# The key projection of a graph attention kernel by features instead of by edges, and a changed first stage

## The chip, the cores and the metric

The kernel runs on one core of one Trainium2 chip. The metric is the device time of one execution in microseconds. Before the change three runs took 2660.58, 2667.97 and 2672.92 us, with the median 2667.97. One further execution was profiled: 2659.95 us.

## The reference

12500 nodes with 128 features, 212500 edges sorted by their destination `dst`. Attention has 8 heads of 16 features:

```
h = relu(layernorm(x))
q = h @ Wq.T + bq ;  v = h @ Wv.T + bv              # per node
k = edge_attr @ Wk.T + bk                            # per edge
qs, qd = q[src], q[dst]
in_m, out_m, diag_m = sum(qs*k), sum(qd*k), sum(qs*qd)   # per head
score = (softmax(in_m/4) + softmax(out_m/4) + softmax(diag_m/4)) * edge_weight**lam
h = segment_sum(score * v[dst], dst)                 # the softmaxes run over the edges of one dst
out = x + leaky_relu(h @ Wo.T + bo, 0.1)
```

The input lam is 1.0, and the kernel skips the power when it is.

## The kernel before

**Cutting up the edges.** The edges are cut into 415 blocks of 512 (128 partitions by 4 columns, JN = 4) and 20 edges left over, the "few". The blocks form S = 5 streams of G = 83 blocks. The loop (line 1754) takes one block of each stream in turn, so five iterations g make one cycle t, s = g % 5.

**The first stage** (to about 157 us in the profile) normalizes the nodes, multiplies them by Wq and writes the query table to DRAM (L1017, L1021). It turns the destinations into bf16 numbers that later make the one-hot matrices, and loads weights and biases. SP's queue carries most of its transfers. It also begins GpSimd's work: indirect gathers fetch the source's row for each edge, four DMAs of 128 rows per block (L713), from the raw x for the first 24 blocks and from the query table afterwards. 29 blocks are gathered ahead of the loop, and then the 20 edges left over, with one gather for their sources and one for their destinations (L743).

The key bias is handled in the first stage. A reflection per head (`bring_to_size`, `reflect`, small VectorE operations and a square root on ScalarE) turns the features of q and of k alike, which leaves their products unchanged, in such a way that the bias of each head falls into one feature, its "lead". Wq, Wk and bq are turned with it.

**The loop, per block g.** The order on each engine is the order in which the code is written: `pin` chains every instruction to the one before it on the same engine.
- TensorE: `turn(g+2)` transposes a block of edge features into PSUM (`eT_ps`, one buffer), ScalarE copies it (`eT`, three buffers). `project(g+1)` multiplies: four matmuls with a slice of eT as the stationary operand and Wk moving, each in two passes (float32), and one small bf16 matmul that adds the lead bias (L1329). k stands in PSUM with edges on partitions (`k_ps`, two buffers). `spread_q(g+1)` selects the destinations' queries by four one-hot matmuls (`qd_ps`, two buffers), which ScalarE copies to `qd`.
- ScalarE: the eT copy, two activations that make the one-hots for g+3 (L704, L705), the qd copy (L1340).
- VectorE: `logits(g)`, three products into one tile of 128x1536 (L1348 qs*k, L1349 qs*qd, L1350 qd*k) and one reduction (L1351).
- A tail that depends on s: scans for the running maxima, exponentials, and w_ps, the weighted sums (L1507), for cycles t-1 to t-3.
- GpSimd: `gather(g+26)`, four DMAs. Line 717 holds them behind TensorE: rows 0 and 1 wait for the last instruction of `project(g)`, issued in the iteration before (`behind[g, 0]`), and rows 2 and 3 wait for the last TensorE instruction of the tail of that iteration (`behind[g, 2]`).
- SP: one load of edge features (`ea`, six buffers, 256 KB), windows of the query table, and stores.

Two iotas on GpSimd (L1698, L1700) at g = 4 and an operation at g = 7 make the selection matrix `shows`.

The lines behind these names:

```
713   rows = pin(nc.gpsimd.indirect_dma_start(out=qq[:, j, :], ...
717   held = behind.get((g - LOOK, j), held)          # LOOK = 26
1320  transpose(eT_ps[:, j, :], ea ...)     1322 eT <- eT_ps (ScalarE)
1328  matmul(k_ps[:, j, :], eT[:, j, :], wk)  1329 k_ps += bias of the leads
1337  matmul(qd_ps[:, j, :], one-hot, window) 1340 qd <- qd_ps (ScalarE)
```

## Time and profile before

| | before |
|---|---|
| three runs | 2660.58, 2667.97, 2672.92 us |
| profiled execution | 2659.95 us, its span 2658.2 us |
| granted TensorE clock, mean | 0.756 |
| gathers from the query table (L713) | 1564, 947 ns each |
| block reduction (L1351) | 415, 1753 ns each |

The first row of the page gives busy time, share of the span and number of instructions of each engine: PE is TensorE's matmul, PEld its weight loads (they overlap with matmuls), DVE is VectorE, ACT ScalarE, POOL GpSimd. In the groups, "busy, mean of one | idle time of the engine just ahead of them, and what ended most of it" follows the shapes. "issue" is time in which an engine waited for nothing that the profile shows; "remote" in the waits is a release that the profile can't name. TensorE's clock changes between 0.5 and 1.0 of full speed during the execution.

### The profile page before, as it was taken

What the parts mean: (1) busy time and instruction counts of PE and PEld (TensorE: products, weight loads), DVE (VectorE), ACT (ScalarE), POOL (GpSimd) and SP (SyncE); (2) the same over time, 40 slices, a digit from 0 to 9 for tenths busy, and PEclk for the clock granted to TensorE, in tenths of its full rate; (3) what the DMA queues carried; (4) which work ended last, traced back from release to release, by engine and by line L of the source; (5) the groups of instructions that cost most, each with busy time, mean ns of one, the idle gap of its engine ahead of it and who ended that gap; (6) DMA issues with size and microseconds to landing.
All of it is one profiled execution on the core that took longest, in us unless ns stands there. A gap on an engine that the chain in (4) does not pass through costs nothing.

```text
span 2658.2 us, 37064 instructions
## 1 busy us (share of the span) xinstructions
PE 1798.2 (68%) x10958; PEld 1457.9 (55%) x10958; DVE 2037.4 (77%) x2835; ACT 1408.4 (53%) x2744; POOL 1587.1 (60%) x1683
## 2 busy tenths in 40 slices
PE   3766766666667667666676677667767676677785
PEld 2455655555555555555555555555555565556674
DVE  4658877777777778787777877777877787777995
ACT  3657754554455555554555555555555555555672
POOL 6655666666666666666666666666666666666100
PEclk7778878777777777776777777777777777667786
DMA  6665455455545554455445544554455445454431
GB/s 187 171 188 156 126 130 145 130 135 137 146 134 136 141 149 128 137 144 145 119 128 134 139 123 130 133 135 126 124 135 131 131 131 132 132 137 123 126 88 53
DMA packets 379842, 357.08 MB, mean 134 GB/s; under 512 B 193358, under 2 KB 299640, under 8 KB 379426
## 3 DMA queue, kind: packets, MB, share of 16 engines
q1 hardware_dynamic: 310720, 239.37, 32.0%
q0 software_dynamic: 53184, 108.92, 16.8%
q10 hardware_dynamic: 15728, 6.33, 1.0%
q8 instruction: 90, 1.47, 0.2%
q14 instruction: 120, 0.98, 0.1%
HBM read 322.16 MB, written 32.22 MB: 133 GB/s over the span
## 4 chain that ended last, share of the span: by engine, by line
PE 44%; issue 16%; DVE 14%; ACT 14%; another core or an unknown queue 8%; DVEq 1%; DMA 1%; POOL 0%; ACTq 0%; SPq 0%
PE k_ps L1328 12%; PE eT_ps L1320 8%; PE w_ps L1507 7%; PE qd_ps L1337 4%; PE m_ps L1451 3%; ACT qd L1340 3%; ACT eT L1322 2%; DVE prod L1349 2%; DVE lT L1351 2%; PE node_ps L1259 2%; DVE prod L1350 2%; DVE prod L1348 2%; ACT relb L704 2%; PE k_ps L1329 2%
## 5 line engine op out<-in xcount | busy, mean ns | idle before, releaser
L713 POOL DMA_INDIRECT qq<-q_table,sources x1564 | 1480.4, 947 | 846.4 <-issue 359.4
L1351 DVE TENSOR_REDUCE lT<-prod 128x96 f32<-128x1536 f32 x415 | 727.4, 1753 | 14.3
L1328 PE MATMUL k_ps<-wk,eT 128*128 128x128 f32 x3320 | 609.4, 341 | 63.5 <-issue 32.2
L1320 PE MATMUL eT_ps<-ident,ea 128*128 128x128 f32 x1660 | 349.4, 345 | 384.1 <-issue 260.9
L1328 PEld LDWEIGHTS k_ps<-wk,eT 128*128 128x128 f32 x3320 | 556.5, 252 | 93.2 <-issue 46.7
L1340 ACT COPY qd<-qd_ps 128x512 f32<-128x512 f32 x415 | 239.5, 577 | 536.2 <-remote 154.7
L1320 PEld LDWEIGHTS eT_ps<-ident,ea 128*128 128x128 f32 x1660 | 240.2, 175 | 479.4 <-issue 315.1
L1348 DVE TENSOR_TENSOR prod<-qq,k_ps 128x512 f32<-128x512 f32 x412 | 280.4, 681 | 206.4 <-PE eT_ps L1320 51.7
L1322 ACT COPY eT<-eT_ps 128x512 f32<-128x512 f32 x415 | 242.8, 585 | 261.3 <-remote 125.3
L1349 DVE TENSOR_TENSOR prod<-qq,qd_ps 128x512 f32<-128x512 f32 x412 | 281.4, 683 | 92.9 <-ACT qd L1340 57.5
L704 ACT ACTIVATE relb<-relb,before 126x512 bf16<-126x512 bf16 x415 | 302.6, 729 | 0.0
L1507 PE MATMUL w_ps<-back,sel 128*126 128x144 f32 (+1 forms) x1296 | 207.8, 325 | 113.3 <-ACT sel L1497 86.1
L1350 DVE TENSOR_TENSOR prod<-qd,k_ps 128x512 f32<-128x512 f32 x415 | 281.8, 679 | 0.0
L705 ACT ACTIVATE oh<-relb 126x512 bf16<-126x512 bf16 x415 | 261.4, 630 | 13.2
L1507 PEld LDWEIGHTS w_ps<-back,sel 128*126 128x126 f32 (+1 forms) x1296 | 189.9, 218 | 126.7 <-ACT sel L1497 96.9
L1337 PE MATMUL qd_ps<-win,oh 126*128 126x128 bf16 x1660 | 199.6, 252 | 16.0 <-issue 14.7
L1337 PEld LDWEIGHTS <-oh 126*128 126x128 bf16 x1660 | 112.2, 109 | 41.3 <-issue 16.9
L1460 DVE TENSOR_TENSOR back<-lT,m_ps 128x480 f32<-128x480 f32 x83 | 54.0, 651 | 93.5 <-remote 36.4
L1451 PE MATMUL m_ps<-ident,m 120*128 120x120 f32 x332 | 74.4, 359 | 67.0 <-issue 39.7
L1411 DVE TENSOR_TENSOR_SCAN l_ps<-far,carry,l_ps 120x512 f32<-120x512 bf16 x80 | 102.5, 1281 | 20.7 <-PE h_ps L1379 6.7
L713 POOL DMA_INDIRECT qq<-in_x_dram,sources x84 | 81.4, 969 | 46.9 <-issue 22.4
L1439 DVE TENSOR_TENSOR_SCAN m<-far,head,l_ps 120x512 f32<-120x512 bf16 x81 | 102.9, 1270 | 0.0
(263 smaller groups left out, 1802.6 us busy)
## 6 DMA issues: line engine op xcount, KB each, us to landing
ea<-in_edge_attr_dram SPq DMA_DIRECT2D x415, 256.0 KB
relb<-rel_d SPq DMA_DIRECT2D x83, 630.0 KB
qq<-q_table,sources POOLq DMA_INDIRECT x1564
win<-q_table SPq DMA_DIRECT2D x415, 31.5 KB
far<-far_d SPq DMA_DIRECT2D x84, 135.0 KB
q_table<-q SPq DMA_DIRECT2D x24, 384.0 KB
sums<-rows SPq DMA_DIRECT2D x411, 7.9 KB
q_table<-xq SPq DMA_DIRECT2D x24, 256.0 KB
```

Of the source, the lines that this page charges most:

```text
L704: pin(nc.scalar.activation(d, d, AF.Abs, bias=before[:K3]))
L713: rows = pin(nc.gpsimd.indirect_dma_start(out=qq[:, j, :], out_offset=None, in_=x if g < RAW else q_table, in_offset=bass.IndirectOffsetOn ...
L1320: pin(nc.tensor.transpose(eT_ps[:, j, :], eas[g][:, j * F:(j + 1) * F], ident))
L1322: pin(nc.scalar.copy(eT, eT_ps))
L1328: pin(nc.tensor.matmul(k_ps[:, j, :], eTs[g][:, j, :], wk, start=(j == 0), stop=False))
L1337: pin(nc.tensor.matmul(qd_ps[:, j, :], ohs[g][:, j * P:(j + 1) * P], d["win"][:, s, :], start=(j == 0), stop=(j == JN - 1)))
L1340: pin(nc.scalar.copy(qds[g], qd_ps))
L1348: pin(nc.vector.tensor_mul(prod[:, :, 0, :], qqs[g], ks[g]))
L1349: pin(nc.vector.tensor_mul(prod[:, :, 1, :], qqs[g], q_ps[g]))
L1350: pin(nc.vector.tensor_mul(prod[:, :, 2, :], qds[g], ks[g]))
L1351: pin(nc.vector.tensor_reduce(lTs[t][:, :, s, :], prod.rearrange("p j i (h d) -> p j (i h) d", d=DIM), AX.X, ALU.add))
L1507: pin(nc.tensor.matmul(w_ps[:(hi - lo) * W, lo:hi].rearrange("p s c -> p (s c)"), d["sel"][:n, j, lo:hi, :].rearrange("p s w -> p (s w)"), ...
```

## The change

**In the loop** the projection runs the other way. `project` is one matmul with Wk as the stationary operand and all 512 columns of eT moving, and gives k by features, `kT_ps` (features on partitions, one PSUM buffer). ScalarE copies it with `bk` as a bias per partition. `turn_back` then transposes it by four matmuls into `k_ps`, with edges on partitions as before. So the reflection is gone, with the matmul for the bias. PSUM has one buffer for each of eT_ps, kT_ps and qd_ps, and two for k_ps; eT has two buffers in SBUF instead of three. An iteration runs turn_back(g+1), spread_q(g+1), project(g+2) and turn(g+3), and the hold for gather rows 0 and 1 stands behind spread_q(g+1). The qs*qd product is VectorE's first of the three.

**In the first stage** lam is loaded as one number (the broadcast load is inside the branch that is skipped), the nine loads of block bounds move to iterations 1 to 6 of the loop, and the loads of biases and bases move to other turns. The selection matrix comes from two small VectorE operations on an index table instead of the two iotas. The few edges are gathered by one DMA of 40 rows, and SP moves the second 20 in iteration 1.

TensorE's order for one iteration in the loop, s = 4, names as in the lists above; before the change:

```order
L1320 MATMUL eT_ps<-ident,ea 128x128 x4
L1328 MATMUL k_ps<-wk,eT 128x128 x4
L1329 LDWEIGHTS ones_92
L1329 MATMUL k_ps<-b_98,ones_92 128x32
L1337 LDWEIGHTS oh
L1337 MATMUL qd_ps<-win,oh 128x128
...
L1507 MATMUL w_ps<-back,sel 126x144 x4
L1507 MATMUL w_ps<-back,sel 84x96 x4
L1371 MATMUL l_ps<-ident,lT 120x128 x4
```

and in the same place after it (L1283 is `turn_back`, L1290 `spread_q`, L1275 `project`, L1268 `turn`):

```order
L1283 MATMUL k_ps<-ident,kT 128x128 x4
L1290 LDWEIGHTS oh
L1290 MATMUL qd_ps<-win,oh 128x128
...
L1275 MATMUL kT_ps<-eT,wk 128x512
L1268 MATMUL eT_ps<-ident,ea 128x128 x4
L1460 MATMUL w_ps<-back,sel 126x144 x4
L1460 MATMUL w_ps<-back,sel 84x96 x4
L1324 MATMUL l_ps<-ident,lT 120x128 x4
```

The transpose of edge features moved from the front of an iteration to the place ahead of the tail; k for the next block, made of ScalarE's kT, stands in front.

ScalarE's order for the iterations s = 3 and s = 4, before:

```order
L1322 COPY eT<-eT_ps 128x512
L704 ACTIVATE relb<-relb,before 126x512
L705 ACTIVATE oh<-relb 126x512
L1340 COPY qd<-qd_ps 128x512
L1496 ACTIVATE sel<-d_ps 128x420 x2
L1497 ACTIVATE sel<-sel 128x840
```

and after:

```order
L705 ACTIVATE relb<-relb,before 126x512
L706 ACTIVATE oh<-relb 126x512
L1293 COPY qd<-qd_ps 128x512
L1278 ACTIVATE kT<-kT_ps,bk_col 128x512
L1270 COPY eT<-eT_ps 128x512
L1449 ACTIVATE sel<-d_ps 128x420 x2
L1450 ACTIVATE sel<-sel 128x840
```

The eT copy moved behind the qd copy, and the new kT copy stands between them.

GpSimd's order at the end of the first stage, before:

```order
L713 DMA qq<-q_table,sources 128x128 x20
L743 DMA qq<-q_table,few_i 20x128 x2
L713 DMA qq<-q_table,sources 128x128 x8
L1698 IOTA ends_ab 21x840
L1700 IOTA ends_ab 1x840
L713 DMA qq<-q_table,sources 128x128 x1536
```

and after:

```order
L859 UNCONDITIONAL_BRANCH x2
L714 DMA qq<-in_x_dram,sources 128x128 x40
L714 DMA qq<-q_table,sources 128x128 x20
L755 DMA qq<-q_table,few_i 40x128
L714 DMA qq<-q_table,sources 128x128 x1544
```

One gather of 40 rows stands where two of 20 stood, and the two iotas are gone from between the loop's gathers.

The core of the diff:

```diff
-    bk_lead = b3[:, 1, None, 0::DIM].to_broadcast([3, JN, HEADS])
+    show_end = consts.tile([K4, S * JN], F32, name="show_end")
+    nc.vector.tensor_scalar(show_end, jp[:K4, 1:K4], 0.0, -1.0, op0=ALU.is_equal, op1=ALU.mult)
+    show_row = consts.tile([1, W], F32, name="show_row")
+    nc.vector.tensor_copy(show_row, jp[0:1, 1:W + 1])
...
-        for i in range(2):
-            pin(nc.gpsimd.indirect_dma_start(
-                out=few["q"][:, i, :], out_offset=None, in_=q_table,
-                in_offset=bass.IndirectOffsetOnAxis(ap=few["i"][:, i:i + 1], axis=0)))
+        pin(nc.gpsimd.indirect_dma_start(
+            out=rows[:, 0, :], out_offset=None, in_=q_table,
+            in_offset=bass.IndirectOffsetOnAxis(ap=few["i"], axis=0)))
+        return rows
+
+    def part_few(rows):
+        pin(nc.sync.dma_start(rows[:EL, 1, :], rows[EL:, 0, :]))
...
-        pin(nc.sync.dma_start(lam_sb, lam[None, :].to_broadcast([RW, 1])))
+        pin(nc.sync.dma_start(lam_sb[0:1, :], lam[None, :]))
...
         with tc.If(lam_v != 0x3F800000):
+            nc.sync.dma_start(lam_sb, lam[None, :].to_broadcast([RW, 1]))
...
-        side = {2: [load_b], 4: [load_bases], 8: [cast_dst], 9: [mark, mark_heads], 10: [store_far], 11: [near_due],
+        side = {5: [load_b], 8: [cast_dst], 9: [mark, mark_heads, load_bases], 10: [store_far], 11: [near_due],
...
-        for s in range(S + 1):
-            beside(12 + s, load_bounds, s)
...
-        bring_to_size()
...
-            if g == -2:
-                reflect()
...
-            eT = work.tile([P, JN, P], F32, name="eT", bufs=3)
+            eT = work.tile([P, JN, P], F32, name="eT")
...
         def project(g):
+            kT_ps = ps.tile([P, JN, P], F32, name="kT_ps", bufs=1)
+            pin(nc.tensor.matmul(kT_ps.rearrange("f j p -> f (j p)"), wk,
+                                 eTs.pop(g).rearrange("f j p -> f (j p)"), start=True, stop=True))
+            kTs[g] = work.tile([P, JN, P], F32, name="kT")
+            pin(nc.scalar.activation(kTs[g], kT_ps, AF.Identity, bias=bk_col))
+
+        def turn_back(g):
             k_ps = ks[g] = ps.tile([P, JN, F], F32, name="k_ps", bufs=2)
             for j in range(JN):
-                pin(nc.tensor.matmul(k_ps[:, j, :], eTs[g][:, j, :], wk, start=(j == 0), stop=False))
-            pin(nc.tensor.matmul(k_ps.rearrange("p j (h d) -> p j h d", d=DIM)[:, :, :, 0], ones3, bk_lead,
-                                 start=False, stop=True))
-            del eTs[g]
+                pin(nc.tensor.transpose(k_ps[:, j, :], kTs[g][:, j, :], ident))
+            del kTs[g]
...
-            qd_ps = q_ps[g] = ps.tile([P, JN, F], F32, name="qd_ps", bufs=2)
+            qd_ps = q_ps[g] = ps.tile([P, JN, F], F32, name="qd_ps", bufs=1)
...
+            pin(nc.vector.tensor_mul(prod[:, :, 1, :], qqs[g], q_ps[g]))
             pin(nc.vector.tensor_mul(prod[:, :, 0, :], qqs[g], ks[g]))
-            pin(nc.vector.tensor_mul(prod[:, :, 1, :], qqs[g], q_ps[g]))
...
         turn(0)
         project(0)
+        turn(1)
+        turn_back(0)
         spread_q(0)
-        turn(1)
+        project(1)
+        turn(2)
...
+            if g + 1 < end:
+                turn_back(g + 1)
+                one_hots(g + 3)
+                spread_q(g + 1)
+                behind[g + 1, 0] = pinned[products]
             if g + 2 < end:
-                turn(g + 2)
-            one_hots(g + 3)
-            if g + 1 < end:
-                project(g + 1)
-                behind[g + 1, 0] = pinned[products]
-                spread_q(g + 1)
+                project(g + 2)
+            if g + 3 < end:
+                turn(g + 3)
             logits(g)
...
+                if t == 0:
+                    part_few(rows_few)
...
-            if g == 4:
-                show_places()
-            elif g == 7:
+            if 0 < g <= S + 1:
+                load_bounds(g - 1)
+            if g == 7:
                 show()
```

More of the change, by code (lines that the diff above doesn't have):

```diff
@@ L972, in turn_w @@
         def turn_w(i, to):
             w_ps = prep_ps.tile([P, F], F32, name="t_ps")
-            if i in (0, 2):
-                pin(nc.tensor.matmul(w_ps, w_in[:, i, :], axes, start=True, stop=True))
-            else:
-                pin(nc.tensor.transpose(w_ps, w_in[:, i, :], ident))
+            pin(nc.tensor.transpose(w_ps, w_in[:, i, :], ident))
             pin(nc.scalar.copy(to, w_ps))
@@ L1868, in ordered_path @@
             halves_of(ab, engine)
-        places_o = [ps.tile([P, JN, F], F32, name="eT_ps", bufs=1)]
-        for r in range(2):
-            places_o += [ps.tile([P, JN, F], F32, name=name, bufs=2) for name in ("k_ps", "qd_ps")]
+        places_o = [ps.tile([P, JN, F], F32, name=name, bufs=n) for name, n in
+                    (("eT_ps", 1), ("kT_ps", 1), ("k_ps", 2), ("k_ps", 2), ("qd_ps", 1))]
         for r in range(len(rest) + 2):
```

101 lines of the change are left out of this document (26 added, 75 removed).

## The prediction

> **What bounds the kernel now.** I first read the page for the load of each engine.
>
> ```profile
> PE 1798.2 (68%) x10958; PEld 1457.9 (55%) x10958; DVE 2037.4 (77%) x2835; ACT 1408.4 (53%) x2744; POOL 1587.1 (60%) x1683
> L713 POOL DMA_INDIRECT qq<-q_table,sources x1564 | 1480.4, 947 | 846.4 <-issue 359.4
> ```
>
> No engine is full, VectorE at 77% the nearest to it, so no busy time explains the span, and I looked for a rate and for what sets it. One reduce (L1351, VectorE) ends the scores of each block, so its count in a window counts blocks. The columns are window, length, busy time, count, granted clock, DMA share, GB/s.
>
> ```profile
> 2000.00:2400.00 400.00, 120.93 (x69) 0.72 0.49 130
> 2500.00:2570.00 70.00, 27.75 (x16) 0.80 0.41 114
> 1700.00:1760.00 60.00, 17.44 (x10) 0.67 0.51 136
> 1450.00:1510.00 60.00, 17.53 (x10) 0.83 0.50 127
> ```
>
> A block takes 5.8 us in the loop (400 / 69), and 4.4 us in the window after 2500 (70 / 16). What is absent there is GpSimd's gathers, whose last is issued at 2477.69. TensorE's clock does not matter: a stretch at 0.67 and one at 0.83 both hold 10 blocks. The timeline of GpSimd and that of ScalarE show the coupling (start, length, then idle time before and what ended it).
>
> ```profile
> 2222.98 0.94 POOL L713 DMA_INDIRECT qq<-q_table,sources  x1 [1.74 <-PE qd_ps L1337]
> 2229.22 0.94 POOL L713 DMA_INDIRECT qq<-q_table,sources  x1 [0.30 <-issue]
> 2231.73 0.94 POOL L713 DMA_INDIRECT qq<-q_table,sources  x1 [1.57 <-PE m_ps L1451]
> 2477.69 0.95 POOL L713 DMA_INDIRECT qq<-q_table,sources  x1 [0.30 <-issue]
> ```
>
> ```profile
> 2222.68 0.41 ACT L1512 COPY rows<-w_ps 126x144 f32<-126x144 f32 x2 [3.74 <-PE qd_ps L1337]
> 2225.28 0.60 ACT L1322 COPY eT<-eT_ps 128x512 f32<-128x512 f32 x1
> 2231.55 0.59 ACT L1340 COPY qd<-qd_ps 128x512 f32<-128x512 f32 x1 [4.39 <-PE m_ps L1451]
> ```
>
> From 2222.98 to 2230.16 six gathers go out back to back, 1.25 us apart (0.94 and 0.30). The chain of waits for that stretch shows TensorE's side:
>
> ```profile
> 2223.63 0.66 PE eT_ps L1320 x4
> ...
> 2225.33 0.33 PE qd_ps L1337 x4
> 2225.94 0.65 PE eT_ps L1320 x4
> ...
> 2228.01 0.33 PE qd_ps L1337 x4
> 2228.34 1.34 issue
> ```
>
> The qd copy that ScalarE starts at 2231.55 needs the matmuls that ended at 2225.66, yet it starts 5.9 us later, after the row of gathers is over at 2230.16. So I read: while GpSimd issues gathers back to back, TensorE's completions reach the others late, and they come out together some 1.4 us after the last gather. GpSimd itself stops because its gathers are held behind TensorE (lines 717 to 721), so each round is some gathers and one stall. Before the loop the same is seen at full size: the 20 last gathers of the first stage and the two of L743 go out in one row that ends at 181.5, and the next scores start after it.
>
> ```profile
> 180.60 0.91 POOL L743 DMA_INDIRECT qq<-q_table,few_i  x1 [0.30 <-issue]
> 166.23 1.75 DVE L1351 TENSOR_REDUCE lT<-prod 128x96 f32<-128x1536 f32 x1
> 185.39 0.69 DVE L1348 TENSOR_TENSOR prod<-ends_ab,k_ps 128x512 f32<-128x512 f32 x1 [17.41 <-remote]
> ```
>
> The table of waits sizes the rounds (us in total, times, longest).
>
> ```profile
> POOL qq L713 <- issue: 381.8, 1242, 1.0
> POOL qq L713 <- remote: 130.5, 76, 2.9
> POOL qq L713 <- PE qd_ps L1337: 83.4, 55, 2.2
> POOL qq L713 <- PE eT_ps L1320: 65.4, 45, 2.3
> POOL qq L713 <- PE k_ps L1329: 63.4, 33, 4.8
> POOL qq L713 <- PE m_ps L1451: 32.4, 22, 1.8
> POOL qq L713 <- PE h_ps L1379: 21.8, 19, 1.7
> ```
>
> The "issue" row is the ordinary step, 381.8 / 1242 = 0.31 us. The other six are stalls: 250, together 396.9 us, 1.59 each, or 1.29 above the step. The loop issues gathers for 386 of its 415 blocks, so 77 cycles of five blocks, with 250 / 77 = 3.25 stalls each. A cycle is then 20 x 1.247 = 24.94 us of gathers (0.947 and 0.30) and 3.25 x 1.29 = 4.19 us of stalls, 29.1 us. The window 2000 to 2400 says 5 x 400 / 69 = 29.0. **The sum rests on these two terms: gathers, and rounds per cycle.**
>
> **The change, part by part.** First the work in the loop.
>
> ```profile
> L1328 PE MATMUL k_ps<-wk,eT 128*128 128x128 f32 x3320 | 609.4, 341 | 63.5 <-issue 32.2
> L1320 PE MATMUL eT_ps<-ident,ea 128*128 128x128 f32 x1660 | 349.4, 345 | 384.1 <-issue 260.9
> L1329 PE MATMUL k_ps<-b,ones 3*128 3x32 bf16 x415 | 91.5, 220 | 3.6 <-issue 3.6
> L1627 PE MATMUL rest_ps<-q_in,ident 128*128 128x512 f32 x32 | 23.0, 811 | 11.3 <-ACT hT L1254 10.4 <-issue 0.9
> L1322 ACT COPY eT<-eT_ps 128x512 f32<-128x512 f32 x415 | 242.8, 585 | 261.3 <-remote 125.3
> ```
>
> - TensorE loses the eight passes of L1328 (609.4 / 415 = 1.47 us per block) and the bias of L1329 (0.22). It gains one product 512 wide, in two passes like those of L1627 (23.0 / 16 = 1.44 for two), and four turns back, which are what L1320 is (349.4 / 415 = 0.84). Net +0.59 us per block, estimated from busy times that overlap. Bounds: 0 (the wide passes stream as the eight small ones do) and +0.77 (two at 0.811).
> - ScalarE gains one copy with a bias, 128x512 from PSUM, 0.585 us as in L1322: 243 us in all, 53% to 62%. VectorE does the same four operations, two of them in another order: 0.
> - Neither fills its engine. With TensorE busy 1798.2 / 415 = 4.3 us per block over the whole span, +0.59 makes 4.9 of 5.8. So by busy time alone the loop costs nothing more; GpSimd's rounds hide it. What that costs without the cover is 386 x 0.59 = 228 us.
>
> The dear part is the hand-overs between engines. In before, TensorE's first work of an iteration is turn(g+2); that copied by ScalarE is all that the next iteration's turn and product need. In the stretch above this let it go through two iterations (2223.63 to 2228.34) after one release, with its buffers doubled (qd_ps, k_ps), until it stood. In the changed kernel, an iteration begins with turn_back(g+1), which needs kT from ScalarE, which needs the product of the iteration before, its third piece of four; the product needs the fourth, eT. And spread_q(g+1) has one qd_ps, so it waits for VectorE's first product and ScalarE's copy of the same block. When completions are late, TensorE can finish one iteration and then must wait for the next release. An iteration allows four gathers (rows 0 and 1 behind one point, rows 2 and 3 behind its end), so the round shrinks towards four gathers: five stalls per cycle, 24.94 + 5 x 1.29 = 31.4 us, or +2.26 us, which over 77 cycles is +174. The other end is rounds as now, +0. Completions within the first two microseconds of a row of gathers still come through (the eT copy of the turn that ended at 2224.29 ran at 2225.28), so some rounds will reach further than four. I take 4.5 stalls, nearer the tight end because the third piece lies late in the iteration: 1.25 x 1.29 x 77 = **+124 us**.
>
> The first stage and the start of the loop:
>
> ```profile
> 18.58 23.14 issue
> 168.04 17.32 another core or an unknown queue
> 197.30 1.24 POOL L1698 IOTA ends_ab<- 21x840 f32 x1
> 198.48 1.19 POOL L1700 IOTA ends_ab<- 1x840 f32 x1
> 29.21 2.99 SPq L820 DMA_DIRECT2D lam_sb<-in_L_gnn_lam_dram  x1
> ```
>
> - One gather of 40 rows for two of 20: one step less in the row that ends at 181.5, 0.91 + 0.30 = 1.2 us. Its second half must then be moved by SP, one small transfer in iteration 1, long before its use in iteration 6.
> - No iotas: 1.24 + 1.19 = 2.4 us of GpSimd, partly time in which it would have stood. Between 0 and -2.4.
> - lam, 2.99 us in SP's queue while the stage stands for 23.14 us: between 0 and -3. The bounds and the bases leave SP's queue in the first stage for later; the nine bounds transfers go one per iteration ahead of that iteration's end, before the tests that read them (iteration 21 on). Nobody waits for them: 0. So too the reflection's some 25 small operations on VectorE: TensorE's 23.14 us from 18.58 on come after them, and I take those for a row of gathers too, which does not move.
> - The edges' rows come one iteration less ahead. No row of the waits names that transfer as a releaser in the loop: 0.
> - The pipeline fills through one more product, copy and turn before the first scores. If these fall into the row of 20 gathers, the two blocks done before it (the second ends at 166.23 + 1.75) are done after it: 0 to 2 x 4.4 = 8.8 us.
>
> I take -4 and +4, so **0** for this part, with 10 us either way.
>
> The sum: profiled execution 2659.95 us, of which 2658.2 is the span, + 124 + 0 = **2784 us**, rounded to 2785. The profiled execution is 8 us (0.3%) under the median of the three runs, 2667.97, so against that it is +117, or 4.4%.
>
> **The rivals.**
>
> *Faster: the rounds grow.* The point that holds rows 0 and 1 moves from behind TensorE's thirteenth pass of an iteration to behind its eighth; k and qd are made ahead of all that serves later blocks, and three weight loads per block go. For it: the stalls are GpSimd waiting for TensorE, and VectorE gets both its inputs by mid-iteration. Against it: turn_back's input is late. It decides below 3.25 stalls per cycle; with 2.3 it is 0.95 x 1.29 x 77 = -94: 2566 us. Half of that is 2613.
>
> *Nothing moves.* The releases are set by GpSimd's stalls alone, and TensorE's +0.59 and ScalarE's +0.585 lie inside the 5.8 us. Only the first stage's few microseconds remain: 2655 us. For it: blocks keep the same pace at both clocks, so the pace does not hang on TensorE's length. Against it: that pace does hang on how far TensorE gets between releases.
>
> *TensorE becomes the bound through its clock.* If the clock stayed at half, TensorE's busy time per block, 4.9 us at the 0.72 of the window 2000 to 2400, would grow by at most 0.72 / 0.5 = 1.44, and by 2 / 1.5 = 1.33 if half of it is at half speed now: 6.5 us against 5.8, over 386 blocks +270: 2930 us, and less where part of a pass does not follow the clock. Against it: nothing in this trace ties the clock to the kind of pass. [...] No view here tells the clock of the turns apart from that of the other passes.
>
> **How the numbers follow.** Forecast (rounds shrink) 0.54; faster 0.25; nothing moves 0.14; clock 0.07. Its own range is 2700 (0.4 of a stall more per cycle) to 2860 (five stalls, 2834, each 0.07 longer since ScalarE has one copy more after a release). For 8 in 10 I go down to 2600, which takes in no change and half of the faster case, and up to 2875. About 0.5% (13 us) is what this kernel's measurement can tell from no change. Slower than that: 0.54 + 0.07, less 0.02 for a forecast that shrinks to nothing, 0.59; within 0.5%: 0.14; faster: 0.27, since the first stage's savings alone could reach beyond 13 us.
>
> **What would show it.** Right: 29.0 us per cycle becomes 30.5 or more between 2000 and 2400, with more than 300 stalls of L713's successor and a mean round under five gathers; TensorE's idle time moves ahead of the turns back, released by kT; after the last gather a block still takes some 4.4 to 4.6 us. Wrong: fewer than 250 stalls, or a cycle of 29 us with the new work hidden, or a clock under 0.65 with TensorE over 85% busy; or if blocks without gathers get slower too, since then the cause is not the gathers.

## The result and the profile after

The changed kernel takes 2687.06 us (median of 6 runs, 2681.65 to 2692.57); the kernel before, in 6 runs beside it, 2668.99 us (2660.58 to 2672.92). The ratio is 1.0086 with a 95% interval of 1.0070 to 1.0101: **slower by 18 us, 0.9%.** The forecast was slower by 117 us against the median. The sign was right, the size was not.

The profiled execution took 2681.65 us, its span is 2679.8 us, 21.6 more than before. Its page shows the busy times and the groups that the change made (L714 is the gather, L1275 the product, L1283 the turn back, L1278 ScalarE's copy with the bias, L1290 spread_q, L1301 VectorE's first product).

```profile
PE 1830.3 (68%) x9711; PEld 1259.4 (47%) x9711; DVE 2018.3 (75%) x2813; ACT 1658.7 (62%) x3158; POOL 1585.4 (59%) x1680
L714 POOL DMA_INDIRECT qq<-q_table,sources x1564 | 1481.6, 947 | 870.5 <-issue 372.5
L1275 PE MATMUL kT_ps<-eT,wk 128*128 128x512 f32 x830 | 614.4, 831 | 71.2 <-issue 42.2
L1283 PE MATMUL k_ps<-ident,kT 128*128 128x128 f32 x1660 | 330.1, 333 | 421.1 <-ACT kT L1278 306.3
L1278 ACT ACTIVATE kT<-kT_ps,bk_col 128x512 f32<-128x512 f32 x415 | 286.2, 690 | 152.3 <-issue 56.9
L1290 PE MATMUL qd_ps<-win,oh 126*128 126x128 bf16 x1660 | 199.4, 255 | 204.2 <-DVE prod L1301 118.1
```

TensorE's idle time did move to where the forecast put it: 421.1 us ahead of the turns back, 306.3 of them released by kT, and 204.2 us ahead of spread_q, 118.1 released by VectorE's first product. TensorE's mean clock rose from 0.756 to 0.799. But the rate of blocks hardly moved (L1304 is VectorE's reduction, one per block):

```profile
2000.00:2400.00 400.00, 117.62 (x68) 0.79 0.50 131
2500.00:2570.00 70.00, 28.05 (x16) 0.93 0.40 114
```

68 blocks in 400 us stand against 69, so a cycle of five blocks takes 29.4 us (5 x 400 / 68) against 29.0. The starts of this reduction cut the span into stretches, in us:

```
                              before    after   difference
start to block 0               159.2    157.2     -2.0
block 0 to 5                    42.8     48.8     +6.0
block 5 to 30                  155.5    159.3     +3.8
block 30 to 380               2072.1   2080.1     +8.0
block 380 to 414               167.3    174.6     +7.3
block 414 to the end            61.2     59.8     -1.4
span                          2658.2   2679.8    +21.6
```

So 350 blocks, in which the forecast wanted some +112, cost 8. The first 30 blocks (9.8) and the last 34, when the gathers are ending or over (7.3), cost about as much each.

### The profile page after: what moved, and what is told of

The parts are those of the page before. It is cut to its first block, busy times and chain, and to the rows that moved or that the text cites. A ratio compares the mean times of both kernels' runs of the same rounds, so it can differ in the third digit from the quotient of the medians.

```text
span 2679.8 us, 35579 instructions
## 1 busy us (share of the span) xinstructions
PE 1830.3 (68%) x9711; PEld 1259.4 (47%) x9711; DVE 2018.3 (75%) x2813; ACT 1658.7 (62%) x3158; POOL 1585.4 (59%) x1680
## 4 chain that ended last, share of the span: by engine, by line
PE 34%; DVE 18%; ACT 16%; issue 14%; another core or an unknown queue 10%; POOL 3%; DMA 3%; DVEq 1%; SPq 1%; ACTq 0%; POOLq 0%
PE kT_ps L1275 10%; PE eT_ps L1268 5%; PE k_ps L1283 4%; DVE lT L1304 4%; POOL qq L714 3%; PE qd_ps L1290 3%; DVE prod L1301 3%; ACT kT L1278 3%; ACT qd L1293 3%; ACT relb L705 3%; PE w_ps L1460 2%; DVE prod L1302 2%; DVE prod L1303 2%; DMA qq<-q_table,sources 2%
## 5 line engine op out<-in xcount | busy, mean ns | idle before, releaser
L714 POOL DMA_INDIRECT qq<-q_table,sources x1564 | 1481.6, 947 | 870.5 <-issue 372.5
L1304 DVE TENSOR_REDUCE lT<-prod 128x96 f32<-128x1536 f32 x415 | 727.5, 1753 | 14.3
L1275 PE MATMUL kT_ps<-eT,wk 128*128 128x512 f32 x830 | 614.4, 831 | 71.2 <-issue 42.2
L1283 PE MATMUL k_ps<-ident,kT 128*128 128x128 f32 x1660 | 330.1, 333 | 421.1 <-ACT kT L1278 306.3
L1283 PEld LDWEIGHTS k_ps<-ident,kT 128*128 128x128 f32 x1660 | 226.4, 168 | 504.5 <-ACT kT L1278 344.5
L1268 PEld LDWEIGHTS eT_ps<-ident,ea 128*128 128x128 f32 x1660 | 271.8, 177 | 328.1 <-issue 320.7
L1301 DVE TENSOR_TENSOR prod<-qq,qd_ps 128x512 f32<-128x512 f32 x412 | 280.2, 680 | 168.7 <-ACT qd L1293 107.9
L1278 ACT ACTIVATE kT<-kT_ps,bk_col 128x512 f32<-128x512 f32 x415 | 286.2, 690 | 152.3 <-issue 56.9
L1290 PE MATMUL qd_ps<-win,oh 126*128 126x128 bf16 x1660 | 199.4, 255 | 204.2 <-DVE prod L1301 118.1
L1268 PE MATMUL eT_ps<-ident,ea 128*128 128x128 f32 x1660 | 322.8, 330 | 2.9 <-DVE att_t L870 2.8
L1290 PEld LDWEIGHTS <-oh 126*128 126x128 bf16 x1660 | 148.8, 116 | 250.2 <-DVE prod L1301 117.4
L1275 PEld LDWEIGHTS kT_ps<-eT,wk 128*128 128x128 f32 x830 | 167.5, 250 | 82.6 <-issue 51.1
L1460 PE MATMUL w_ps<-back,sel 128*126 128x144 f32 (+1 forms) x1296 | 160.8, 278 | 10.1 <-issue 8.8
L1460 PEld LDWEIGHTS w_ps<-back,sel 128*126 128x126 f32 (+1 forms) x1296 | 153.3, 182 | 16.3 <-issue 13.5
L714 POOL DMA_INDIRECT qq<-in_x_dram,sources x84 | 81.8, 973 | 43.0 <-issue 22.6
```

Source lines behind the costliest of these rows:

```text
L714: rows = pin(nc.gpsimd.indirect_dma_start(out=qq[:, j, :], out_offset=None, in_=x if g < RAW else q_table, in_offset=bass.IndirectOffsetOn ...
L1268: pin(nc.tensor.transpose(eT_ps[:, j, :], eas[g][:, j * F:(j + 1) * F], ident))
L1275: pin(nc.tensor.matmul(kT_ps.rearrange("f j p -> f (j p)"), wk, eTs.pop(g).rearrange("f j p -> f (j p)"), start=True, stop=True))
L1278: pin(nc.scalar.activation(kTs[g], kT_ps, AF.Identity, bias=bk_col))
L1283: pin(nc.tensor.transpose(k_ps[:, j, :], kTs[g][:, j, :], ident))
L1290: pin(nc.tensor.matmul(qd_ps[:, j, :], ohs[g][:, j * P:(j + 1) * P], d["win"][:, s, :], start=(j == 0), stop=(j == JN - 1)))
```

## The stops of the gathers, before and after

I took each distance between two gathers over 1.35 us, after 300 us, as a stop, and what is above the ordinary step of 1.247 us as its length:

```
                    stops   gathers between   mean stop   total us   stop after rows of 2 / 4 / 6 / 8 / 10
before                243        6.06           1.386       336.9       1.12  1.01  1.37  1.70   -
after                 276        5.34           1.275       352.0       1.01  1.03  1.35  1.67  2.01
```

There are more stops, 20 / 5.34 = 3.75 per cycle instead of 3.30, but nothing near 4.5, and 33 stops more cost 15 us in all, 0.46 us each instead of 1.29. For the most part a stop is shorter after a shorter row: a line through the rows of 4, 6 and 8 is about 0.35 us plus 0.17 us per gather in both kernels. The rows of two don't lie on it, which would give them 0.7 us.

The rows did not shrink to four either: in the changed kernel 88 have six gathers, 52 eight and 21 ten. They became less even: rows of one to three gathers went from 22 to 69, and rows of eight from 87 to 52. One of ten, in the timelines of GpSimd, TensorE and ScalarE (start, length; idle time ahead and its releaser in brackets):

```profile
1438.28 0.94 POOL L714 DMA_INDIRECT qq<-q_table,sources  x1 [1.79 <-PE kT_ps L1275]
...
1449.51 0.94 POOL L714 DMA_INDIRECT qq<-q_table,sources  x1 [0.30 <-issue]
1452.77 0.94 POOL L714 DMA_INDIRECT qq<-q_table,sources  x1 [2.32 <-remote]
```

```profile
1440.79 1.07 PE L1283 MATMUL k_ps<-ident,kT 128*128 128x128 f32 x4 [1.84 <-ACT kT L1278]
...
1442.08 2.02 PE L1275 MATMUL kT_ps<-eT,wk 128*128 128x512 f32 x2
1443.89 0.80 PE L1268 MATMUL eT_ps<-ident,ea 128*128 128x128 f32 x4
1444.53 0.60 PE L1199 MATMUL node_ps<-ident,h 128*128 128x128 f32 x4
1444.97 0.60 PE L1283 MATMUL k_ps<-ident,kT 128*128 128x128 f32 x4
```

```profile
1444.14 0.69 ACT L1278 ACTIVATE kT<-kT_ps,bk_col 128x512 f32<-128x512 f32 x1 [1.11 <-issue]
1446.83 0.58 ACT L1270 COPY eT<-eT_ps 128x512 f32<-128x512 f32 x1 [2.01 <-issue]
1452.44 0.58 ACT L1202 COPY hT<-node_ps 128x512 f32<-128x512 f32 x1 [5.02 <-remote]
```

The product that ends at 1444.10 is copied at 1444.14, 5.9 us into the row: on time. The turn that ends at 1444.69 is copied 2.1 us late, and the matmuls that end at 1445.13 only 7.3 us later, when the row is over. So in this row completions are not held from its start: kT still gets through, and TensorE makes its second iteration (1444.97) in the same row. The prediction allowed that only for completions in the first two microseconds.

## The experiments

Two theories stood: "rounds" (the prediction's: 1.29 us per stop) and "gathers" (from the table above: 0.41 us per stop by a line through all rows, and 0.16 us for each gather ahead of it). One fact has to be told ahead of them, since no number can be understood without it: the jobs ran on three chips, which the record numbers 0, 4 and 8. On chip 0 the kernel before takes 2660 us, about as above (the runs of the result carry no number; I count them with chip 0). On chips 4 and 8 it takes 2163 to 2164 us, and in `half_again`, which has the same time on chip 4, the stops are all but missing (24 of 0.29 us). Every ratio is against the kernel before in the same job and on the same chip.

### Chip 0: the holds

`hold_end`:

```diff
-                behind[g + 1, 0] = pinned[products]
...
-            behind[g + 1, 2] = pinned[products]
+            behind[g + 1, 0] = pinned[products]
```

> The kernel before, with all four gather rows of a block held behind one point, the end of TensorE's iteration before (rows 0 and 1 were held behind the product of that iteration). Theory 'rounds' (the prediction's): every stop of the gathers costs 1.29 us whatever it follows, so rounds forced down to four gathers, 5 stops per cycle instead of 3.25, cost +2.26 us per cycle, +174 us in 77 cycles. Theory 'gathers' (from the two traces, where a stop lasts about 0.35 us plus 0.17 us for each gather of the row before it): a gather costs 1.42 us wherever the stops lie and a stop only 0.35 us, so 1.6 stops more per cycle cost 0.56 us, +43 us.

Measured: 2707.73 us against 2660.23, ratio 1.0187 (1.0165 to 1.0208), +47.5 us. That is the number of the theory "gathers", but not by its way: the rows were not cut to four. 138 of 221 had eight gathers and 66 four; the mean row grew to 6.64, and the stops grew to 1.71 us, 1.74 after rows of four where before has 1.01. The total of the stops, 378.5 us against 336.9, is +41.6 and accounts for most of the time. So the length of the row ahead doesn't set the stop by itself. I read it as the least length, to which a hold that opens late adds; no run tests that. Both theories had the wrong premise, that one hold per block makes rows of four.

`hold_loose`:

```diff
-                held = behind.get((g - LOOK, j), held)
+                held = behind.get((g - LOOK - 1, j), held)
```

> The kernel before, with every gather held behind TensorE's instruction of one iteration earlier than now, so that GpSimd may run one block further ahead of TensorE. Theory 'rounds': rows of 8 to 10 gathers instead of 6, 2 to 2.5 stops per cycle, -75 to -125 us. Theory 'gathers': the stops become longer in the same measure, and only 0.35 us per saved stop is won, -27 to -38 us, or nothing where VectorE runs dry in the longer rows.

Measured: 2668.16 us, 1.0033 (1.0014 to 1.0051), +8 us. Neither theory. The stops stayed as they were (248, 1.367 us each, after 5.91 gathers). GpSimd did run one block further: when VectorE starts a block's reduction, 26 later blocks are gathered instead of 25, from block 50 to block 380. There it stands at its holds in the same rhythm, so a hold one iteration earlier makes no longer rows.

### Chip 0: the two parts of the change apart

`first_only` is the kernel before with the diff of the first stage (lam, bounds, biases and bases, index table instead of iotas, one gather of 40 rows and `part_few`), with one `ea` buffer less:

```diff
-    AHEAD, IDX, EDGES = LOOK + FIRST, 8, 6
+    AHEAD, IDX, EDGES = LOOK + FIRST, 8, 5
...
+                if t == 0:
+                    part_few(rows_few)
```

> The kernel before with the first stage's part of the change alone: lam as one number, bounds in the loop, biases and bases later, no iotas, one gather for the last edges; the loop and the reflection stay, and the edge features have five buffers instead of six. If the loop's part makes the 19 us: -2 to -4 us against before. If the moved loads or the small transfer in iteration 1 make the start of the loop slower (blocks 0 to 5 take 6 us longer in the changed kernel): +4 to +8 us.

`loop_only` is the changed kernel with that diff undone:

```diff
-        side = {5: [load_b], 8: [cast_dst], 9: [mark, mark_heads, load_bases], 10: [store_far], 11: [near_due],
+        side = {2: [load_b], 4: [load_bases], 8: [cast_dst], 9: [mark, mark_heads], 10: [store_far], 11: [near_due],
...
-                if t == 0:
-                    part_few(rows_few)
```

> The changed kernel with its first stage's part undone: lam by broadcast, bounds, biases and bases where they were, two iotas, two gathers for the last edges; k by features in the loop and no reflection. If the loop's part makes the 19 us: +20 to +25 us against before. If the first stage's part makes a third of it: +10 to +14 us.

Measured: `first_only` 2662.44 us, 1.0008 (0.9997 to 1.0018); `loop_only` 2687.83 us, 1.0105 (1.0083 to 1.0126), +27.6 us. On this chip the loop's part makes the whole loss, and the first stage's part is worth nothing that can be told from zero. (The changed kernel was not run in this job. Its 2687.06 us are those of `loop_only`, but the kernel before took 2668.99 beside it and 2660.23 here, so 18 and 28 us may be one and the same loss.) The stretches of `loop_only` are those of the changed kernel: +9.8 us between blocks 30 and 380, +8.0 in the last 34 blocks, +5.1 between 5 and 30, +4.2 between 0 and 5.

Where the gathers are over, the waits can be read. Windows of 100 us of each kernel there (the columns are PE, PEld, DVE, ACT, POOL busy with counts, clock, DMA, GB/s), before:

```profile
2490.00:2590.00 100.00, 81.63 (x573) 67.36 (x569) 97.80 (x124) 72.93 (x148) 1.67 (x4) 0.86 0.37 104
```

and after, with the largest wait of TensorE there:

```profile
2510.00:2610.00 100.00, 78.42 (x494) 56.15 (x492) 94.19 (x119) 83.76 (x164) 1.67 (x4) 0.91 0.36 101
...
PE qd_ps L1290 <- DVE prod L1301: 17.4, 12, 3.0
```

VectorE sets the pace there and falls from 97.8% busy to 94.2%. The largest wait of TensorE that is new is the one on the single qd_ps; that it costs VectorE its time is not shown by this.

### Chip 4: half the bytes, a longer step, one qd_ps, spread_q last

`pad`:

```diff
+                if g >= AHEAD + 3:
+                    pin(nc.gpsimd.memset(pad, 0.0))
                 held = behind.get((g - LOOK, j), held)
```

> The kernel before, with a tiny GpSimd memset (128x4) behind each gather of the loop, which makes GpSimd's own step from one gather to the next longer by 0.1 us (such a memset is 98 ns at the start of the trace) up to some 0.2 us. Theory 'rounds': the step of 1.247 us is the gathers' whole price, so 1536 steps more by 0.1 to 0.2 us cost +150 to +300 us. Theory 'gathers': a gather takes 1.41 us of something that goes on behind GpSimd's instruction and is made up for in the stops (0.41 us and 0.16 us per gather); a longer step leaves less to make up for, the stops shrink by as much, and the time moves by 0 to +50 us.

`half_rows` (the table is seen as twice as many rows of half the width, so the kernel leaves out the right rows and half of each; only its time is of use):

```diff
-                    out=qq[:, j, :], out_offset=None, in_=x if g < RAW else q_table,
+                    out=qq[:, j, 0:wide], out_offset=None,
+                    in_=x if g < RAW else q_table if wide == F else q_table.rearrange("n (b f) -> (n b) f", b=2),
```

> The kernel before, in which the loop's gathers fetch rows of half the width, 256 B instead of 512 B, as many of them, and VectorE reads each half row twice (the right rows and the other half are left out). Theory 'gathers', the time is in moving the bytes: the stops lose their 0.16 us per gather, 20 x 0.16 x 77 = -246 us, less where VectorE becomes the bound (4.4 to 4.7 us per block). Theory 'gathers', the time is in the 128 descriptors of each: no change, 0. Theory 'rounds': no change, 0.

`one_qd`:

```diff
-            qd_ps = q_ps[g] = ps.tile([P, JN, F], F32, name="qd_ps", bufs=2)
+            qd_ps = q_ps[g] = ps.tile([P, JN, F], F32, name="qd_ps", bufs=1)
...
-            pin(nc.vector.tensor_mul(prod[:, :, 0, :], qqs[g], ks[g]))
             pin(nc.vector.tensor_mul(prod[:, :, 1, :], qqs[g], q_ps[g]))
+            pin(nc.vector.tensor_mul(prod[:, :, 0, :], qqs[g], ks[g]))
```

> The kernel before with one qd_ps buffer instead of two and VectorE's products in the order of the changed kernel. If the single qd_ps is what costs the changed kernel its 19 to 27 us: in the 34 blocks without gathers about +6 us as there, and +10 to +25 us in all. If the copy of kT and its late hand-over cost it: 0 to +5 us.

`spread_last` (of the changed kernel):

```diff
                 turn_back(g + 1)
-                one_hots(g + 3)
-                spread_q(g + 1)
                 behind[g + 1, 0] = pinned[products]
+                one_hots(g + 3)
             if g + 2 < end:
                 project(g + 2)
             if g + 3 < end:
                 turn(g + 3)
+            if g + 1 < end:
+                spread_q(g + 1)
```

> The changed kernel with spread_q moved behind project and turn in TensorE's and ScalarE's order, and the hold of rows 0 and 1 behind turn_back. If the single qd_ps costs by making TensorE stand in the middle of its iteration: nearer to before, +5 to +15 us against before instead of +19 to +27. If qd's own chain (VectorE's first product, spread_q, ScalarE's copy, VectorE's third product) is what is long: slower than the changed kernel, +40 us or more against before.

This job ran on chip 4, where the kernel before took 2163.93 us. Measured: `pad` 1.0130 (1.0113 to 1.0148), `half_rows` 1.0001 (0.9991 to 1.0011), `one_qd` 1.0038 (1.0024 to 1.0053), `spread_last` 1.0122 (1.0106 to 1.0139). `spread_last` has the moved SP transfer of the changed kernel too (below), so neither of its two cases can be read from +26 us; and `one_qd`, +8 us, lies between its two. No trace of the kernel before was kept on this chip. The kernel `half_rows` can stand for it in what follows, since its time is the same. GpSimd's timeline and the page of its repetition `half_again`:

```profile
999.55 0.94 POOL L714 DMA_INDIRECT qq<-q_table,sources  x1 [0.30 <-issue]
1000.80 0.94 POOL L714 DMA_INDIRECT qq<-q_table,sources  x1 [0.30 <-DVE score L1202]
...
PE 1641.9 (76%) x10958; PEld 1330.8 (62%) x10958; DVE 2004.5 (93%) x2835; ACT 1380.9 (64%) x2744; POOL 1591.8 (74%) x1683
```

The gathers have the same length and step as on chip 0 (0.94 and 0.30), but they run almost without a stop: 24 stops after 300 us, 0.29 us each. So `pad` and `half_rows` could tell nothing of what makes a stop.

Two things differ from chip 0. First, ScalarE is on time. I took how long each qd copy between 400 and 2000 us starts after both the last qd matmuls to end ahead of it and ScalarE's work before it. In the kernel before on chip 0, 97 of 270 copies are over 1 us late, up to 4.7 (126, up to 7.3, from the end of the copy's own matmuls); in `half_again` none of 341 is later than 0.04 us, and on chip 0 none of the 25 behind the last gather. Second, GpSimd is not at its holds. These are the blocks gathered ahead when VectorE starts the reduction of a block:

```
block                     50   100   200   300   350
before (chip 0)           25    25    25    25    25
half_again (chip 4)       23    17     8     1     1
pad_again (chip 4)        22    16     6     1     1
after_again (chip 4)      23    18    12     4     1
after_late (chip 8)       23    19    13     5     1
```

In `half_again` a block takes 4.56 us between blocks 30 and 300, with VectorE busy for 493 of the 500 us from 500 to 1000. Four gathers take 4 x 1.247 = 4.99 us, so the lead is used up. From then on VectorE waits for gathers, and a block takes 5.06 us (blocks 300 to 380). The wait in the window 1550 to 2090, and the last gather in `half_again`, `after_again` and `after_late`:

```profile
DVE prod L1357 <- DMA qq<-q_table,sources: 32.1, 25, 3.3
...
2092.80 0.94 POOL L714 DMA_INDIRECT qq<-q_table,sources  x1 [0.30 <-issue]
...
2120.07 0.94 POOL L714 DMA_INDIRECT qq<-q_table,sources  x1 [0.30 <-issue]
...
2095.87 0.94 POOL L714 DMA_INDIRECT qq<-q_table,sources  x1 [0.30 <-issue]
```

So on this chip GpSimd's row of gathers sets the end, though VectorE shows 93% and GpSimd 74% (the 0.30 us between two gathers count as idle). `pad` shows it: its step is longer, 1.26 us (0.95, 0.12 and 0.19), its gathers end 28 us later, and it costs 27 us.

The same again, with the changed kernel beside it, ran on chip 4 once more:

> The kernel with the tiny memset behind each gather again, since before took 2164 us on the chip of the last four runs, and no stops were seen there. On a chip where before takes some 2660 us: theory 'gathers' (0.16 us per gather made up for in the stops) says the stops shrink by what the step grows (0.02 to 0.1 us each), 0 to +50 us; theory 'rounds' says +30 to +150 us with stops as long as before. On the other chip +27 us again.

> Half the row width again, the rest as told before. On a chip where before takes some 2660 us: -100 to -246 us if the late completions come from the bytes moved, 0 if they come from the number of descriptors or of gathers. On the other chip 0 again.

> One qd_ps in the kernel before again. On a chip where before takes some 2660 us: +10 to +25 us if the single qd_ps is what costs the changed kernel its time, 0 to +5 us if it is kT. On the other chip +8 us again.

> The changed kernel again, beside these. On a chip where before takes some 2660 us: +18 to +27 us as measured. On the other chip, where blocks take 4.7 us and no row of gathers hides TensorE's and ScalarE's added work: 0.21 us per block as in the changed kernel's 34 last blocks would be 386 x 0.21 = +81 us; if instead GpSimd's step (5.0 us per block) is the bound there and hides it, +10 to +30 us.

Measured: 1.0122 (1.0107 to 1.0137), 0.9998 (0.9988 to 1.0007), 1.0039 (1.0025 to 1.0052), and for the changed kernel 2194.82 us against 2164.36, **1.0140 (1.0125 to 1.0156), +30 us.** The second case of its expectation for this chip gives the number, at its edge: GpSimd's step does set the end and hides work of the loop. But most of the 30 us is something that neither case named, as the stretches show (`half_again` stands for before; `after_late`, told below, ran on chip 8):

```
                            half_again  after_again  difference   after_late
start to block 0               128.9       127.9        -1.0        126.2
block 0 to 5                    28.2        48.2       +20.0         26.3
block 5 to 30                  137.1       143.8        +6.7        145.2
block 30 to 380               1637.0      1638.7        +1.7       1636.9
block 380 to 414               167.2       172.1        +4.9        171.0
block 414 to the end            60.8        62.1        +1.3         61.0
span                          2159.2      2192.8       +33.6       2166.6
```

In the first five blocks 20 of the 33.6 us are lost. The timelines of SP, ScalarE and VectorE there, the last gather of the first stage, and SP's wait:

```profile
124.61 0.39 SPq L643 DMA_DIRECT2D sources<-in_src_dram  x1
153.07 0.83 SPq L761 DMA_DIRECT2D qq<-qq  x1
154.12 0.36 SPq L688 DMA_DIRECT2D win<-q_table  x1
154.54 0.80 SPq L737 DMA_DIRECT2D heads<-in_dst_dram  x1
...
150.68 0.92 POOL L755 DMA_INDIRECT qq<-q_table,few_i  x1 [0.31 <-issue]
...
158.00 0.72 ACT L705 ACTIVATE relb<-relb,before 126x512 bf16<-126x512 bf16 x1 [18.51 <-DMA tops<-in_dst_dram]
...
140.03 0.68 DVE L1647 TENSOR_TENSOR qq<-node_ps,bq_all 128x512 f32<-128x512 f32 x1
159.89 0.69 DVE L1301 TENSOR_TENSOR prod<-qq,qd_ps 128x512 f32<-128x512 f32 x1 [19.18 <-ACT qd L1293]
...
SPq L761 <- DMA qq<-q_table,few_i: 28.0, 1, 28.0
```

L761 is `part_few`, the small transfer of the last edges' second 20 rows. It waits for the single gather that fetches them, which stands behind twenty others on GpSimd and is issued at 150.68. From 125 to 153 us SP stands there, and the windows, bounds and edge features of the next iterations go out only behind it. ScalarE is next to be late (18.51 us), then VectorE (19.18). GpSimd's holds behind these blocks open late as well: block 60's gathers start at 338.4 us instead of 313.3, and the 25 us are not made up (the last gather above is 27.3 us late).

### Chip 8: the transfer later

`after_late` (of the changed kernel; `first_late` is the same edit of `first_only`):

```diff
-                if t == 0:
-                    part_few(rows_few)
-                elif t == 1:
+                if t == 1:
                     logits_few()
...
-            if 0 < g <= S + 1:
-                load_bounds(g - 1)
+            if g == 4:
+                part_few(rows_few)
+            if 8 <= g <= S + 8:
+                load_bounds(g - 8)
```

> The changed kernel with two of its moved SP transfers moved again: the transfer that parts the last edges' rows from iteration 1 to iteration 4, and the bounds' loads from iterations 1 to 6 to 8 to 13. In the changed kernel's trace SP stands from 155 to 178 us with that transfer, which waits for the last gather of the first stage, and the loop's windows, edge features and bounds are queued behind it. Theory 'SP queue': blocks 0 to 5 lose their extra time, -15 to -20 us against the changed kernel where before takes 2164 us (so +10 to +15 against before), and -4 to -6 us where before takes some 2660 us (+13 to +20). Theory 'pipeline fill' (one product, copy and turn more before the first scores): no change, +30 and +19 to +27.

> The kernel before with the first stage's part of the change alone, with the same two transfers moved to iteration 4 and to iterations 8 to 13. Theory 'SP queue': the first stage's savings (1 to 4 us) are left, -1 to -5 us against before. If the savings lie in time in which the stage stands anyway: 0.

> The tiny memset behind each gather once more, for a chip where before takes some 2660 us: theory 'gathers' 0 to +50 us with stops shorter by what the step grows, theory 'rounds' +30 to +150 us with stops as long as before. On the other chip +27 us, as twice measured.

Measured against 2163.61 us: `after_late` 2168.34 us, 1.0023 (1.0012 to 1.0033); `first_late` 2162.21 us, 0.9991 (0.9982 to 1.0000); `pad` 1.0142 (1.0122 to 1.0162). A last job repeated it:

> The changed kernel with the two SP transfers later. On a chip where before takes some 2660 us: +13 to +20 us against before if SP's queue costs there too, +19 to +28 us if the late completions of that chip hide it. On the other chip +5 us, as measured there.

> One qd_ps in the kernel before. On a chip where before takes some 2660 us: +10 to +25 us if the single qd_ps is what the loop's part (+28 us there) costs, 0 to +5 us if it is kT's hand-over. On the other chip +8 us, as measured there.

> The tiny memset behind each gather, again for a chip where before takes some 2660 us: theory 'gathers' 0 to +50 us with stops shorter by what the step grows, theory 'rounds' +30 to +150 us with stops as long as before. On the other chip +27 to +31 us, as measured there.

`after_late` 1.0018 (1.0007 to 1.0029), `one_qd` 1.0028 (1.0017 to 1.0040), `pad` 1.0133 (1.0114 to 1.0151).

With the transfer later, SP, and VectorE's fourth block in `after_late`:

```profile
143.04 0.36 SPq L688 DMA_DIRECT2D win<-q_table  x1
155.81 0.82 SPq L761 DMA_DIRECT2D qq<-qq  x1
...
138.95 0.69 DVE L1301 TENSOR_TENSOR prod<-qq,qd_ps 128x512 f32<-128x512 f32 x1 [0.56 <-ACT qd L1293]
```

The block that waited 19.18 us waits 0.56, blocks 0 to 5 take 26.3 us instead of 48.2, the last gather is 3.1 us late instead of 27.3, and the loss falls from 30 us (chip 4) to 4 or 5 (chip 8, where the changed kernel itself was not run). **On these chips five sixths of the change's cost are a transfer of twenty rows that stood in SP's queue (with the bounds behind it)**; both were moved together, so their shares are not told apart. The longer pipeline at the start of the loop, the rival, shows no part in it: `after_late` has it, and its first five blocks take less than the 28.2 us of `half_again`.

What is left, +4 to +5 us, is not more than what one qd_ps alone costs the kernel before in three jobs (+6 to +8 us by the ratios). In the waits of `one_qd_again` TensorE's on that buffer is the longest:

```profile
PE qd_ps L1337 <- DVE prod L1348: 431.6, 261, 8.3
```

The pair is in the changed kernel too (361.7 us in 277 waits in `after_again`). That it makes the 4 to 5 us is not shown, for a second qd_ps in the changed kernel was not tried. Nor is the rebuilt loop free. Between blocks 30 and 300, where VectorE sets the pace, `after_again` takes 1251.5 us, `one_qd_again` 1238.0 and `half_again` 1232.3: the loop costs 19 us there, of which one qd_ps alone makes 6. Between 300 and 380, where in `half_again` the gathers set the pace, `after_again` takes 387.2 us and `half_again` 404.7, and the cost is given back. GpSimd's gathers hide it.

No version beat both kernels clearly. `first_late` came nearest, 1.4 us under before by the medians, with an interval that reaches to 1.

## Why the prediction was wrong, point by point

**The step that failed** is "the round shrinks towards four gathers ... I take 4.5 stalls ... 1.25 x 1.29 x 77 = +124 us". Two of its three factors were off. (1) The number: 3.75 stops per cycle came, 0.45 more than before and not 1.25. TensorE did stand for kT (306.3 us), but 164 of the 276 rows still had six gathers or more. The premise that completions get through only in the first two microseconds of a row was read from one row; in another the copy of kT was on time 5.9 us into it. (2) The price: 1.29 us was the mean of all stops, taken for the price of one more. The 33 stops more cost 15 us, 0.46 us each. In these two traces a stop has some 0.35 us plus 0.17 us for each gather of the row before, and cutting the same gathers into more rows adds only the first term, 12 us for 33. This line fits the two totals; it isn't shown to be the cause, and `hold_end` breaks it (1.74 us after rows of four). The table of waits gave just the sum and the count. Sorting the stops by what went ahead of them would have shown this in the trace of before. (3) `hold_loose` shows that the picture was too simple as well: looser holds made no longer rows.

By its own signs the prediction is wrong too: the cycle stayed at 29.4 us with the new work hidden, and the blocks without gathers got slower. The last 24, all behind the last gather, took 4.62 us each before and 4.80 after.

**The first stage, taken as 0, with "Nobody waits for them: 0" and "one small transfer in iteration 1, long before its use".** The use is late, but the transfer's own wait was not counted, nor what is queued behind it on SP. On chips 4 and 8 that is 26 us by `after_late`. On chip 0 it was hidden: SP stands there from 155 to 178 us too, but VectorE starts its third block only at 182.70,

```profile
177.88 0.83 SPq L761 DMA_DIRECT2D qq<-qq  x1
...
182.70 0.69 DVE L1301 TENSOR_TENSOR prod<-ends_ab,qd_ps 128x512 f32<-128x512 f32 x1 [14.35 <-ACT qd L1293]
```

and before started its third at 185.39, so `first_only` cost nothing there. The range of 10 us for this part held on that chip and not on the others.

**What held.** TensorE's idle time went ahead of the turns back, released by kT, and spread_q waits for VectorE's first product. By busy time nothing filled up: the product took 614.4 / 415 = 1.48 us per block (1.44 estimated), the turns back 0.80 (0.84), and ScalarE's copy with the bias 0.69 (0.585 estimated, the copy without one). TensorE's busy time grew by 32 us only, nearer to the lower bound of 0 than to +0.59 per block; at a higher clock its other work got shorter (the weighted sums, L1507 before and L1460 after, from 207.8 to 160.8 us, with a mean granted clock of 0.77 and 0.95 during them). 16 blocks without gathers still fit into 70 us as forecast.

**The rivals.** "Nothing moves" is nearest in the long middle of the loop: 8 us in 350 blocks. "Faster" did not come. The clock's rival is out: the granted clock rose, from 0.756 to 0.799 on chip 0 and from 0.821 (`half_again`) to 0.875 on chip 4, with twice as many turns per block. No run shows a clock that stays at half, the term on which its 2930 us rest: the lowest mean clock of any run was 0.746. As the other passes changed with the turns, what a turn by itself does to the clock is not shown.

**What stays open.** Why ScalarE's copies follow TensorE late on chip 0 while gathers run (97 of 270 by over 1 us), and in `half_again` on chip 4 not (none of 341), with the same 0.94 us gathers at the same step. There the blocks outrun the gathers (4.56 us against 4.99), GpSimd falls behind its holds (from 23 blocks ahead to 1), and there is little to stop it. A price per gather is what chip 0's rows suggest, and no run could settle it, since the runs that change a gather's bytes or its step met the chips without stops. Also open is how the loop's 28 us on chip 0 divide between the single qd_ps and the hand-over of kT: `one_qd` ran on chips 4 and 8 only.

## What to carry to other kernels

A mean over all stops is not the price of one more stop: sort the stops by what went before them, and see which part stays when their number changes. Of a transfer that is moved, ask first when its own source is ready, and then list what is queued behind it until then; a transfer of twenty rows that held up SP's queue, with the bounds behind it, cost some 26 us on chips 4 and 8, and the rebuilt loop 4 to 5. Look for the engine that never stops, and not only for the busiest: GpSimd at 74% set the end on chip 4, and hid what the loop cost VectorE (19 us between blocks 30 and 300). And where the same wait shows in one row of a timeline, look at ten before building a rule on it.

## What the runs showed of the hardware

The same kernel took 2660 us on one chip (0) and 2164 us on two others (4 and 8), 23% apart, with GpSimd's gathers at the same 0.94 us and the same step. On chip 0, rows of gathers are followed by stops of 1 to 2 us, and ScalarE's copies start late while gathers run: 97 of 270 by over 1 us, and one in the changed kernel 7.3 us after its matmuls. On chip 4, 1430 gathers pass with 24 stops of 0.3 us, and none of 341 copies is late. A change that costs 0.9% on the one costs 1.4% on the other, and for another reason. Halving the bytes of the loop's gathers changed neither their 0.94 us nor the time on chip 4 (0.9998, 0.9988 to 1.0007).
